# A two-layer graph network: rows of the middle passes made at the head of the turn that spreads them, and one square root for four blocks in the first pass

## The chip, the cores and the metric

The kernel runs on one core of a Trainium2 chip. A core has five engines with a queue of instructions each: TensorE (PE, matmuls), VectorE (DVE), ScalarE (ACT), GpSimd (POOL) and SyncE (SP), which here only issues DMA transfers. An engine takes its instructions in order; an instruction that has to wait holds up all behind it on its engine. The metric is the device time of one execution in microseconds, the median over several.

## The reference

The input is a table `x` of 32768 rows of 128 f32 numbers and 524288 edges (`src`, `dst`), sorted by `dst`. Two layers follow one another:

```python
# layer 0: x1 = layernorm(x + L0(x))
agg = segment_sum(x[src], dst)           # sums of neighbours' rows
h_local = bn(x + mlp((1 + eps) * x + agg))
h_attn  = bn(x + attention(x))           # 64 groups of 512 rows, 8 heads
L0 = bn(h + ffn(h)),  h = h_local + h_attn
# layer 1: out = layernorm(x1 + L1(x1)), three steps:
q = x @ Wq.T + bq
retrieved = softmax(q @ keys.T) @ values            # 512 keys
agg[row] += (dinv * x)[col];  lap = x - dinv * agg
x = 0.5 * x + 0.5 * (retrieved - 0.2 * lap)
# then layernorm(x, ln_w, ln_b)
```

So each of the three steps of layer 1 is, for each row, `0.4 x + 0.5 retrieved + 0.1 dinv agg`. The edges are the same in all of them.

## The kernel before, in words

The work of layer 1 is cut into 64 blocks of 512 rows (`NB` blocks of `BLK` rows, of `NCH` = 4 chunks of 128). Sums over neighbours are made by exchange through DRAM: rows are *spread* into slots ordered by the window of 128 rows that they go to, written to DRAM (`slots`), and in the next pass read back and *summed* per window. Both are matmuls with 0/1 matrices. So layer 1 is four passes:

- the first pass (pool `l1p`): makes layer 0's last normalisation, and spreads its rows;
- two middle passes (`l1w`, the loop over `t`): each sums what the pass before has spread, which ends a step, and spreads the new rows;
- the last pass (`l1z`): sums, and makes the two last normalisations.

A pass can't begin its sums before the pass ahead has written its last slots, as a window's slots come from all blocks.

What one block goes through, by the functions that hold it:

- `first` (first pass only): `load` fetches the block of layer 0's output (`vT`) and of the input (`x1`), `scale` applies batch norm on ACT, `turn` transposes on PE and adds on DVE, `norm` is a layer norm: mean and variance on DVE, square root on ACT (L1083), reciprocal and scaling on DVE (L1087, L1089), and a write of the rows to DRAM for the last pass.
- `consume` (middle and last pass): four windows of 19 matmuls each into a PSUM tile `seg` (5 with rows fetched singly by POOL, `listed`, 2 `common`, 12 with slots, `y_i`), each closed by three DVE instructions (L2103) that give the new rows `xn`. The 0/1 matrix of a window, `oh`, is one DVE instruction.
- `prepare`: the rows times `dinv` (`nx`), cut into three bf16 parts on ACT and DVE in turn (`rows`, `split_steps`: cast, subtract, cast, subtract, then a write to DRAM); the transposed rows `xT` (four transposes on PE, a copy on ACT) and the query `qT` (a matmul, then ACT).
- `emit`: scores against the keys, softmax (maximum on DVE, `Exp` on ACT), transposes, the product with the values, and the part of the step that needs no sums, `part_o`, to DRAM; and 24 times `spread`: two matmuls into a two-bank PSUM tile `exp`, and a cast of it to bf16 `y_o` by ACT or DVE (L1449). In the first pass every second cast is DVE's, in the middle passes every fourth. After each three casts SP writes half a window's slots.

There are two `exp` tiles in PSUM, so a pair of spreading matmuls waits for the cast of the pair before the last. In the middle passes there is one PSUM tile for query and scores together, and one for transposes.

The loop runs in turns, one block further each. In the first pass of before, turn n loads block n+3, does `first` of block n+2, `prepare` of block n+1 and `emit` of block n. In a middle pass, turn n sums block n+2, prepares block n+1 and spreads block n. Each step has a place number; `placed` sorts the steps of a turn by it, `weave` mixes the sums' steps evenly between them. This is the order of tracing. The order in each engine's queue is then set by a scheduler that works with priorities in order of tracing and its own estimates of readiness; layer 0 and the last pass switch it off (`manual_schedule`), the first and middle passes don't.

`Sqrt` and `Exp` lie in different tables of ACT; the compiler puts a table load ahead of each change.

Of the kernel before, what the change touches and what calls it, by code (L numbers as in the profile page):

```python
# [9 lines left out]
F32 = mybir.dt.float32  # L10
# [3 lines left out]
AF = mybir.ActivationFunctionType  # L14
OP = mybir.AluOpType
# [4 lines left out]
P = 128  # L20
D = 128
BLK = 512
NCH = BLK // P
# [885 lines left out]
def tile_gnn_resnorm(ctx: ExitStack, tc: tile.TileContext, a: dict, out: bass.AP):  # L909
# [8 lines left out]
    nc = tc.nc  # L918
    N = a["x"].shape[0]
    E = a["src"].shape[0]  # L920
    NB = N // BLK
# [38 lines left out]
    eps_c = cp.tile([P, 1], F32, name="eps_c")  # L960
# [9 lines left out]
    v = {n: vec[:, k:k + 1] for k, n in enumerate(VECS)}  # L970
# [984 lines left out]
    def layer1_grid(v_d, s3, c3):  # L1955

        exs = [Exchange("src", slots_d[t % 2], rows_d[t]) for t in range(T_STEPS)]
        with tc.tile_pool(name="l1g", bufs=1) as gp:
# [6 lines left out]
                if w < NW:  # L1965
                    picked[w] = exs[0].known_pick(wp, w)

            def first(b, st, wp, p_tr):


                def load():
                    st["v"] = wp.tile([P, BLK], F32, name="vT")
                    nc.sync.dma_start(st["v"], v_d[b])
                    st["x0"] = wp.tile([P, NCH, D], F32, name="x1")
                    nc.sync.dma_start(st["x0"], rows_of(a["x"], b))

                def scale():
                    nc.scalar.activation(st["v"], st["v"], AF.Identity, bias=c3, scale=s3)

                def turn():  # L1980
                    st["x"] = wp.tile([P, NCH, D], F32, name="xn", bufs=5)
# [10 lines left out]
            def prepare(t, b, st, wp, p_s, p_tr):  # L1992

                ex = exs[t]

                def rows():
                    nx = wp.tile([P, NCH, D], F32, name="nx")
                    nc.vector.tensor_tensor(nx, st["x"], dinv[:, b * NCH:(b + 1) * NCH].unsqueeze(2)
                                            .to_broadcast([P, NCH, D]), OP.mult)
                    st["r"], st["split"] = ex.split_steps(wp, b, nx, nx)  # L2000

                def project():
                    ps = p_tr.tile([P, NCH, P], F32, name="tr")
                    for c in range(NCH):
                        nc.tensor.transpose(ps[:, c, :], st["x"][:, c, :], ident)
                    st["xT"] = wp.tile([P, BLK], F32, name="xT")
                    nc.scalar.copy(st["xT"], ps.rearrange("p c n -> p (c n)"))

                def query():
                    ps = p_s.tile([P, BLK], F32, name="s")  # L2010
                    nc.tensor.matmul(ps, w["WqT"], st["xT"], start=True, stop=True)
# [121 lines left out]
            with tc.tile_pool(name="l1p", bufs=2) as wp, \  # L2133
                    tc.tile_pool(name="l1p_exp", bufs=2, space=PSUM) as p_e, \
                    tc.tile_pool(name="l1p_s", bufs=2, space=PSUM) as p_s, \
                    tc.tile_pool(name="l1p_tr", bufs=2, space=PSUM) as p_tr:
                sts, firsts = {}, {}
                for w0 in range(2):
                    ask_pick(wp, w0)
                for n in range(-3, NB):  # L2140
                    b = n + 3
                    if b < NB:
                        sts[b] = {}
                        load, firsts[b] = first(b, sts[b], wp, p_tr)
# [36 lines left out]
            with tc.tile_pool(name="l1z", bufs=2) as wp, \  # L2181
                    tc.tile_pool(name="l1z_r", bufs=1, space=PSUM) as p_r, \
                    tc.tile_pool(name="l1z_seg", bufs=4, space=PSUM) as p_g:
                t = T_STEPS - 1
                ramp = ramp_in_psum(p_r)
                with tc.manual_schedule():
# [3 lines left out]
                    for b in range(NB):  # L2190
                        st = {}
# [84 lines left out]
```

## Time and profile before

| | |
|---|---|
| median of 3 runs | 13,724.5 us (13,710.27 to 13,725.8) |
| profiled execution, its own time | 13,720.72 us |
| its span, first to last instruction | 13,718.8 us |
| granted TensorE clock, mean | 0.948 |
| PE busy over the span | 85% |
| DVE, ACT, POOL busy | 74%, 49%, 39% |

The stages of the span, in microseconds from its start, by the first and last instruction of each: attention, sorting of the edges and layer 0 until 6250; the first pass of layer 1 from 6256 to 7708; the two middle passes to 9883 and to 12,027; the last pass to the end.

How to read the lines of the profile: a group is line, engine, operation, output and inputs, shapes and count, then busy microseconds and the mean nanoseconds of one, then the idle time of the engine ahead of these instructions and what ended it. A wait line names who waited for whom, the sum in microseconds, how often, and the longest. A timeline line begins with start and length in microseconds. An f32 matmul appears as two rows. A matmul's end is modelled, and matmuls overlap, so their starts say more than their lengths.

### The profile page before, as it was taken

Reading aid. Unit: us, or ns where it says so; the run is one execution under the profiler, and the core shown is the slowest. Engines: PE = TensorE matmul, PEld = TensorE weight load, DVE = VectorE, ACT = ScalarE, POOL = GpSimd, SP = SyncE. Lnnn points to the kernel's source line nnn. Section 1 sums busy time; section 2 is a strip of 40 time slices with the busy share of each in tenths; the row PEclk is TensorE's granted clock in tenths of the full one; section 3 lists DMA queues with packets and bytes.
Section 4 is the critical chain, followed back from the end, with each engine's and each line's share of the span. In section 5 each row is a group of like instructions: output and inputs, shape, how many; then the busy total and the mean of one; then the engine's idle time right before and its main releaser. Section 6 shows DMA issues by size and latency. Waiting matters only on the chain. (4 is left out here: it accounts for less than half of the span.)

```text
span 13718.8 us, 167775 instructions
## 1 busy us (share of the span) xinstructions
PE 11728.4 (85%) x58924; PEld 5767.8 (42%) x58984; DVE 10087.5 (74%) x16572; ACT 6762.4 (49%) x10444; POOL 5314.5 (39%) x5333
## 2 busy tenths in 40 slices
PE   8988898887777888888999799999899999966666
PEld 3333333333333444444444455555455555533333
DVE  6998898879997777767888666666566666566666
ACT  4444444448884111137888566666566666600000
POOL 0000000000003777720000366666566666567777
PEclk9999999999999999999999999999999999988777
DMA  1000000007778999967888899999999999988887
GB/s 41 13 11 12 18 13 11 14 34 277 273 294 312 314 314 315 314 229 261 304 311 310 315 402 401 398 399 399 357 400 400 398 398 401 378 302 289 288 291 256
DMA packets 1339021, 3590.33 MB, mean 262 GB/s; under 512 B 197298, under 2 KB 579154, under 8 KB 1337010
## 3 DMA queue, kind: packets, MB, share of 16 engines
q1 hardware_dynamic: 968816, 2936.78, 56.6%
q0 software_dynamic: 252608, 520.41, 11.9%
q10 hardware_dynamic: 116738, 122.29, 2.6%
q8 instruction: 465, 7.62, 0.2%
q14 instruction: 394, 3.23, 0.1%
HBM read 2075.81 MB, written 1502.97 MB: 261 GB/s over the span
## 5 line engine op out<-in xcount | busy, mean ns | idle before, releaser
L1462 POOL DMA_INDIRECT listed<-rows,other x5120 | 5169.1, 1010 | 4103.9 <-issue 3140.6
L1449 ACT CAST y_o<-exp 128x768 bf16<-128x768 f32 x4352 | 3317.6, 807 | 984.7 <-PE exp L1444 732.6
L1444 PE MATMUL exp<-rows,pick 128*128 128x384 bf16 x12288 | 2818.7, 329 | 414.7 <-ACT y_o L1449 247.9
L1487 PEld LDWEIGHTS <-oh 128*128 128x128 bf16 x19456 | 1982.9, 102 | 2664.4 <-issue 1608.4
L1487 PE MATMUL seg<-y_i,oh 128*128 128x384 bf16 x12288 | 2643.7, 346 | 20.0 <-DMA y_i<-slots 18.7
L1449 DVE CAST y_o<-exp 128x768 bf16<-128x768 f32 x1792 | 1711.3, 955 | 688.9 <-PE exp L1444 576.7
L1444 PEld LDWEIGHTS <-pick 128*128 128x128 fp8e4 x12288 | 1203.3, 98 | 2054.3 <-issue 1371.6
L1487 PE MATMUL seg<-listed,oh 128*128 128x384 bf16 (+1 forms) x5120 | 1303.5, 335 | 885.5 <-DMA listed<-rows,other 848.3
L1390 POOL MEMSET rows<- 128x8 bf16 x64 | 6.8, 107 | 4022.2 <-DMA attn_d<-aT 2859.3
L1639 ACT ACTIVATE pT<-s 128x1024 f32<-128x1024 f32 x1024 | 1027.5, 1025 | 999.5 <-PE s L1614 859.7
L2103 DVE SCALAR_TENSOR_TENSOR part_i<-seg,dinv,part_i 128x128 f32<-128x128 f32 x1536 | 532.6, 347 | 1331.9 <-PE seg L1487 1320.8
L1619 DVE TENSOR_REDUCE mx<-s 128x2 f32<-128x1024 f32 x1024 | 1239.9, 1222 | 312.4 <-PE s L1614 308.4
L1614 PE MATMUL s<-k,q 32*128 32x512 f32 x4096 | 1196.7, 665 | 89.3 <-ACT pT L1639 82.0
L1635 PE MATMUL s<-ql,k 32*128 32x512 f32 x4096 | 1129.4, 646 | 63.8 <-DVE ql L1629 36.1
L1083 ACT ACTIVATE ln_rs<-ln_mv,eps_c 128x4 f32<-128x4 f32 x192 | 57.2, 298 | 1642.2 <-DVE ln_mv L1081 1641.5
L2028 PE MATMUL s<-keysT,qT 128*128 128x512 f32 x1536 | 796.0, 600 | 2.7 <-ACT pr L1062 1.7
L1432 DVE TENSOR_SCALAR_CACHE_REDUCE pick<-row_p,lane 128x512 fp8e4<-128x512 f32 x768 | 555.2, 748 | 260.2 <-PE row_p L1421 243.9
L2040 PE MATMUL s<-pt,values 128*128 128x512 f32 x1536 | 725.9, 595 | 10.7 <-ACT pt L2035 10.4
L1473 DVE TENSOR_TENSOR oh<-iota,slot 128x2432 bf16<-128x2432 bf16 x512 | 724.6, 1415 | 3.0 <-DMA slots<-y_o 3.0
L1473 DVE TENSOR_TENSOR oh<-ramp_p,slot 128x2432 bf16<-128x2432 bf16 x512 | 724.2, 1415 | 3.4 <-DMA slots<-y_o 3.4
L1487 PE MATMUL seg<-common,oh 128*128 128x384 bf16 (+1 forms) x2048 | 632.8, 351 | 69.1 <-DMA common<-rows,shared 68.6
L1421 PE MATMUL row_p<-row,ident_b 128*128 128x512 bf16 x1476 | 587.1, 398 | 95.7 <-DVE pick L1806 88.9
(404 smaller groups left out, 14138.6 us busy)
## 6 DMA issues: line engine op xcount, KB each, us to landing
slots<-y_o SPq DMA_DIRECT2D x2048, 576.0 KB
y_i<-slots SPq DMA_DIRECT2D x1024, 1152.0 KB
pick<-pick SPq DMA_DIRECT2D x1024, 192.0 KB
listed<-rows,other POOLq DMA_INDIRECT x5120
rows<-rows SPq DMA_DIRECT2D x192, 384.0 KB
part_d<-part_o SPq DMA_DIRECT2D x192, 256.0 KB
part_i<-part_d ACTq DMA_DIRECT2D x192, 256.0 KB
rows<-rows SPq DMA_DIRECT2D x64, 386.0 KB
```

Of the source, the lines that this page charges most:

```text
L1421: nc.tensor.matmul(ps, gc["ident"][:, w % P:w % P + 1].to_broadcast([P, P]), self.row[:, w // P, j * BLK:(j + 1) * BLK], start=True, stop= ...
L1444: nc.tensor.matmul(ps[:, j, :ROW], pick[:, o:o + P], r, start=True, stop=True)
L1449: (nc.vector.tensor_copy if to_dve else nc.scalar.copy)(dst, ps[:, :, :ROW])
L1462: nc.gpsimd.indirect_dma_start(out=g[:, k, :], out_offset=None, in_=self.table, in_offset=bass.IndirectOffsetOnAxis(ap=index[:, k:k + 1], ...
L1473: nc.vector.tensor_tensor(oh.rearrange("p c (w z) -> p c w z", z=2), ramp.rearrange("p (w z) -> p w z", z=2)[:, None].to_broadcast([P, NC2 ...
L1487: nc.tensor.matmul(ps[:, :n], oh[:, j, :], src, start=(k == 0), stop=(k == NC2 - 1))
L1614: nc.tensor.matmul(ps[:, s % 2, :], t["q", o][32 * s:32 * s + 32, c * P:(c + 1) * P], t["k", o][32 * s:32 * s + 32, :], start=True, stop=True)
L1619: nc.vector.tensor_reduce(m[:, c, 2 * i:2 * i + 2, xr[o]], st[b].pop(("two", i)), AX.X, OP.max, negate=True)
L1635: nc.tensor.matmul(ps[:, s % 2, :], t["k", o][32 * s:32 * s + 32, c * P:(c + 1) * P], t["ql", o][32 * s:32 * s + 32, :], start=True, stop= ...
L1639: nc.scalar.activation(t["p", c][:, 2 * i:2 * i + 2, :], ps, AF.Exp)
L2028: nc.tensor.matmul(s, st["q"][:, c * P:(c + 1) * P], keysT, start=True, stop=True)
L2040: nc.tensor.matmul(ps, values[:, k, :], st["pt"][:, k, :], start=(k == 0), stop=(k == NCH - 1))
```

## The change

There are two changes, in the first pass and in the middle passes.

In the first pass, `norm` is cut in two. `moments` makes mean and variance of a block into a tile that holds four blocks, and with the fourth block makes one square root and one reciprocal for all of them (16 columns). `norm` scales a block by them. So that the four blocks are there, the loop begins with turn -7 instead of -3: turn n loads block n+7, does `scale`, `turn` and `moments` of block n+6, `norm` of block n+2, and `prepare` and `emit` as before. `vT` has three buffers, `x1` eight.

In the middle passes turn n now sums block n+1, and both prepares and spreads block n. All steps of `prepare` come ahead of `emit`'s, in the order rows, the four steps of the split, transposes, query. There are 65 turns instead of 66 in a pass.

```diff
-            def first(b, st, wp, p_tr):
+            def first(b, st, wp, p_tr, group):
+                k = b % NCH
...
+                def moments():
+                    if k == 0:
+                        group["mv"] = wp.tile([P, NCH, NCH, 2], F32, name="ln_mvs")
+                    st["mv"] = group["mv"]
+                    t = wp.tile([P, NCH, 6], F32, name="ln_st")
+                    for c in range(NCH):
+                        nc.vector.bn_stats(t[:, c, :], st["x0"][:, c, :])
+                        nc.vector.bn_aggr(st["mv"][:, k, c, :], t[:, c, :])
+                    if k == 0:
+                        group["rs"] = wp.tile([P, NCH, NCH], F32, name="ln_rss")
+                    st["rs"] = group["rs"]
+                    if k == NCH - 1:
+                        nc.scalar.activation(st["rs"], st["mv"][:, :, :, 1], AF.Sqrt, bias=eps_c)
+                        nc.vector.reciprocal(st["rs"], st["rs"])
+
                 def norm():
-                    layer_norm(wp, st["x0"], st["x"])
+                    st["x"] = wp.tile([P, NCH, D], F32, name="xn", bufs=5)
+                    for c in range(NCH):
+                        nc.vector.tensor_scalar(st["x"][:, c, :], st["x0"][:, c, :], st["mv"][:, k, c, 0:1],
+                                                st["rs"][:, k, c:c + 1], op0=OP.subtract, op1=OP.mult)
                     nc.sync.dma_start(kept_of(xs_d[0], b), flat(st["x"]))
-                return load, [(7, scale), (12, turn), (15, norm)]
+                return load, [(7, scale), (12, turn), (15, moments)], [(14, norm)]
...
+                if at_once:
+                    return [(-1, f) for f in (rows, lambda: st["split"][0](), lambda: st["split"][1](),
+                                              lambda: st["split"][2](), lambda: st["split"][3](), project, query)]
                 return [(1, rows), (2, project), (4, lambda: st["split"][0]()), (7, query),
...
-                for n in range(-3, NB):
-                    b = n + 3
+                for n in range(-NCH - 3, NB):
+                    b = n + NCH + 3
...
-                    if n + 2 in sts:
-                        lists.append(firsts.pop(n + 2))
-                    if n + 1 in sts:
+                    if n + NCH + 2 in firsts:
+                        lists.append(firsts.pop(n + NCH + 2))
+                    if n + 2 in norms:
+                        lists.append(norms.pop(n + 2))
+                    if 0 <= n + 1 < NB:
                         lists.append(prepare(0, n + 1, sts[n + 1], wp, p_s, p_tr))
...
-                    for n in range(-2, NB):
+                    for n in range(-1, NB):
                         lists = []
-                        if n + 1 in sts:
-                            lists.append(prepare(t + 1, n + 1, sts[n + 1], wp, p_s, p_tr))
                         if n >= 0:
+                            lists.append(prepare(t + 1, n, sts[n], wp, p_s, p_tr, True))
                             lists.append(emit(t + 1, n, sts[n], wp, p_e, p_s, p_tr, 4))
                         two_b = placed(*lists)
-                        b = n + 2
+                        b = n + 1
```

More of the change, by code (lines that the diff above doesn't have):

```diff
@@ L1966, in ask_pick @@
                     picked[w] = exs[0].known_pick(wp, w)
-            def first(b, st, wp, p_tr):
+            def first(b, st, wp, p_tr, group):
+                k = b % NCH
                 def load():
-                    st["v"] = wp.tile([P, BLK], F32, name="vT")
+                    st["v"] = wp.tile([P, BLK], F32, name="vT", bufs=3)
                     nc.sync.dma_start(st["v"], v_d[b])
-                    st["x0"] = wp.tile([P, NCH, D], F32, name="x1")
+                    st["x0"] = wp.tile([P, NCH, D], F32, name="x1", bufs=2 * NCH)
                     nc.sync.dma_start(st["x0"], rows_of(a["x"], b))
@@ L1980, in turn @@
                 def turn():
-                    st["x"] = wp.tile([P, NCH, D], F32, name="xn", bufs=5)
                     ps = p_tr.tile([P, NCH, P], F32, name="tr")
@@ L1985, in turn, with prepare @@
                     nc.vector.tensor_add(st["x0"], st["x0"], ps)
+                def moments():
[12 more added lines that the diff above has]
+                        nc.vector.reciprocal(st["rs"], st["rs"])
                 def norm():
-                    layer_norm(wp, st["x0"], st["x"])
+                    st["x"] = wp.tile([P, NCH, D], F32, name="xn", bufs=5)
+                    for c in range(NCH):
+                        nc.vector.tensor_scalar(st["x"][:, c, :], st["x0"][:, c, :], st["mv"][:, k, c, 0:1],
+                                                st["rs"][:, k, c:c + 1], op0=OP.subtract, op1=OP.mult)
                     nc.sync.dma_start(kept_of(xs_d[0], b), flat(st["x"]))
-                return load, [(7, scale), (12, turn), (15, norm)]
-            def prepare(t, b, st, wp, p_s, p_tr):
+                return load, [(7, scale), (12, turn), (15, moments)], [(14, norm)]
+            def prepare(t, b, st, wp, p_s, p_tr, at_once=False):
                 ex = exs[t]
@@ L2136, in layer1_grid @@
                     tc.tile_pool(name="l1p_tr", bufs=2, space=PSUM) as p_tr:
-                sts, firsts = {}, {}
+                sts, firsts, norms, group = {}, {}, {}, {}
                 for w0 in range(2):
                     ask_pick(wp, w0)
-                for n in range(-3, NB):
-                    b = n + 3
+                for n in range(-NCH - 3, NB):
+                    b = n + NCH + 3
                     if b < NB:
                         sts[b] = {}
-                        load, firsts[b] = first(b, sts[b], wp, p_tr)
+                        load, firsts[b], norms[b] = first(b, sts[b], wp, p_tr, group)
                         load()
                     lists = []
-                    if n + 2 in sts:
-                        lists.append(firsts.pop(n + 2))
-                    if n + 1 in sts:
+                    if n + NCH + 2 in firsts:
[3 more added lines that the diff above has]
+                    if 0 <= n + 1 < NB:
                         lists.append(prepare(0, n + 1, sts[n + 1], wp, p_s, p_tr))
```

## The prediction

> **What bounds the kernel now.** I read the busy time by stage first, then the groups and waits of the two stages that the diff touches, then the timelines of single turns. A turn is one pass of the loop over blocks of 512 rows. The stages, as microseconds, then busy time and instructions of each engine, clock, DMA share, GB/s:
>
> ```profile
> 6256.00:7708.00 1452.00, 1300.34 (x6002) 689.23 (x6002) 1252.41 (x2342) 1271.70 (x2103) 0.00 (x0) 1.00 0.84 305
> 7708.00:9883.00 2175.00, 2075.41 (x10638) 1159.39 (x10639) 1309.08 (x2115) 1352.17 (x2240) 1416.77 (x1341) 0.99 1.01 390
> 9883.00:12027.00 2144.00, 2059.82 (x10610) 1152.99 (x10610) 1302.68 (x2110) 1352.78 (x2241) 1355.38 (x1283) 1.00 1.01 392
> ```
>
> In the first pass PE, DVE and ACT are all at 86 to 90%: three engines that hand two PSUM buffers (`exp`) round, none of them full. In the middle passes PE is at 95%. The groups of the first pass on ACT, and what DVE waits for there:
>
> ```profile
> L1062 ACT ACT_TABLE_LOAD x63 | 80.8, 1283 | 1.1
> L1083 ACT ACT_TABLE_LOAD x62 | 79.5, 1283 | 1.1
> ...
> L1083 ACT ACTIVATE ln_rs<-ln_mv,eps_c 128x4 f32<-128x4 f32 x64 | 19.1, 298 | 2.5 <-DVE ln_mv L1081 1.8
> ```
> ```profile
> DVE y_o L1449 <- PE exp L1444: 138.5, 212, 1.7
> DVE nm L1060 <- PE s L2028: 36.3, 71, 1.4
> ```
>
> The reader is to see 125 table loads, two per block (to Sqrt, back to Exp): 160 us of ACT's 1272. ACT's timeline shows how they stand in its queue:
>
> ```profile
> 6918.74 1.28 ACT L1083 ACT_TABLE_LOAD   x1
> 6920.04 0.30 ACT L1083 ACTIVATE ln_rs<-ln_mv,eps_c 128x4 f32<-128x4 f32 x1
> 6920.25 0.80 ACT L1449 CAST y_o<-exp 128x768 bf16<-128x768 f32 x1
> ```
>
> A steady middle turn, PE by start:
>
> ```profile
> 8810.23 1.13 PE L2011 MATMUL s<-xT,w_WqT 128*128 128x512 f32 x2
> 8811.19 1.63 PE L1487 MATMUL seg<-y_i,oh 128*128 128x384 bf16 x9
> ...
> 8815.86 0.81 PE L1444 MATMUL exp<-rows,pick 128*128 128x384 bf16 x4 [0.29 <-ACT y_o L1449]
> 8817.23 0.48 PE L1444 MATMUL exp<-rows,pick 128*128 128x384 bf16 x2 [0.56 <-ACT y_o L1449]
> ```
>
> From start to start a 384-column matmul takes 0.162 us, a 512-column f32 one 0.86, a transpose 0.11. A turn has 76 `seg`, 48 `exp`, 9 f32 products and 24 transposes: 12.3 + 7.8 + 7.7 + 2.6 = 30.4 us. Turns in 8400 to 9400 last 32.7 to 34 (mean 32.9), and what is missing is mostly `exp` waiting for a cast. DMA moves 399 GB/s there, but PE waits for it only 6 us in 1200 (8200 to 9400).
>
> The ends of the passes, on PE:
>
> ```profile
> 7707.49 0.48 PE L1444 MATMUL exp<-rows,pick 128*128 128x384 bf16 x2 [0.72 <-DVE y_o L1449]
> 7719.44 0.48 PE L1487 MATMUL seg<-listed,oh 128*128 128x384 bf16 x1 [11.47 <-DMA listed<-rows,other]
> ...
> 7781.69 0.52 PE L1444 MATMUL exp<-rows,pick 128*128 128x384 bf16 x2
> ```
>
> 74 us pass with no `exp`: 11.5 until the first rows come, then sums of two whole blocks, limited by gathers. In the next pass it is 49.7 us (9882.9 to 9932.65). At the other end, 9821.8 to 9882.9, two blocks are spread with almost no sums beside them.
>
> **The skill.** The page "ScalarE: Activation LUTs", section "What ACT_TABLE_LOAD costs", puts a change of table set at 1283 ns of load plus about 1380 of drain, 2.66 us. The trace has the 1283, but from load to next instruction only 1.30 us (6918.74 to 6920.04); I go by the trace, so half of the page's price. "Perfetto Trace Analysis", section "Identifying the Most-Contended Engine", says that matmul occupancy doesn't measure how full PE is; here one `seg` shows 326 ns while they start 162 apart, so I count starts.
>
> **Part 1, first pass: one Sqrt for four blocks.** Removed: 48 Sqrt (about 0.2 us each from start to start), 48 reciprocals on DVE (0.17), and table loads: the compiled order has 39 where it had 133, so 94 x 1.30 = 122 us off ACT's queue; with the Sqrts 132 us, 2.1 per turn. Added: nothing but longer-lived buffers (`x1` 8, `vT` 3). Moved: loads of `vT` and `x1` (two SP issues of 0.34 us, 256 KB each) go four turns earlier; their buffers are free, so SP's queue doesn't stop. The norms keep their turn, but in the compiled order the norms of a group (16 x 0.25 us) now stand close together on DVE.
>
> What a load costs: laid over all loads from 6660 to 7560, DVE idles 24% of the 1.3 us of the Sqrt load and 25% of the 1.2 after it (0.6 us), 13% of 1.5 us after the Exp load (0.2), and half of the 2 us that begin 6 us after it (1.0), when ACT's casts and exponentials lie back to back. So 0.8 us per turn directly, 1.8 at most. Below, DVE is the floor: 1252/64 = 19.6 us per turn of 22.7. In three turns of four 0.8 to 1.8 goes: 38 to 86 us. I take 60. Late next is DVE. If its bunched norms delay casts, I leave 0 to 30 us of loss in the range. The head: four blocks must be through before the first norm, three more than now, DVE 0.68 + 0.9 + 0.7 us each, some 7 us; the last turns are lighter by the same work: +4. Sum **-56**.
>
> **Part 2, one turn less between sums and spreading (two passes).** *Ends.* First `exp` comes after sums of one block, not two. First middle pass: 11.5 + 28 (four windows, 7719.4 to 7747.5) + 6.5 for the new head below = 46 instead of 74: -28. Second: four windows are done at 9909.65, so 9916 instead of 9932.65: -16. The drain has one lone block instead of two, but one more full turn is run: lone ones take 30 each (61 us for two), a full turn 32.9, and the sums of three quarters of a block are left over where before there were none: before 62 x 32.9 + 2 x 30.5 = 2101 from first to last `exp`, after 62.75 x 32.9 + 1.25 x 30 = 2102. To it come about 5 us for the head of the last block, which nothing covers. -28 + 5 - 16 + 5 = **-34**. The last `rows` write (SP, 384 KB) is issued one turn later, still some 20 us before the pass ends, so the gathers on POOL's queue find it landed.
>
> *Steady turn.* I timed its head by hand along the compiled order, with latencies from the trace (PE to ACT or DVE 0.21, the others 0.05). t = 0 is the last `seg` of the block. DVE closes it with a one-hot (1.33) and a cast between: `xn` at 3.3, `nx` at 3.9. PE meanwhile has 26 `seg` of the next windows and 8 `exp` of the old block. ACT: casts, `rows` at 5.4, `xT` to 6.5; PE, ready at 6.15, waits 0.4 for it. Query to 7.5, `qT` to 8.4; behind two `seg` the first score waits 0.6. Behind `qT` on ACT the second `rows` cast ends at 8.9, DVE's last subtraction at 9.7, just when PE asks for the new rows. With small waits 1.3 us by then, another 0.8 in the rest of the turn, 32.6 in all, where the shortest turns are now 32.7. The jitter of now (mean 32.9) makes it 32.8; f32 products that follow a wait took 0.96 instead of 0.86, and two more of them do so: 33.0; and as I left out casts that wait for a write to `slots`, I take 33.1, +0.2 us per turn, for 126 turns: **+25**; bounds -0.3 (windows now end 8 to 9 us apart, not 4 to 12, which evens the fetches) and +1.0 (the query wait and the score wait both uncovered): -38 to +126.
>
> Sum: -56 - 34 + 25 = -65. The profiled execution took 13,720.7 around a span of 13,718.8; the median is 13,724.5, 4 us above. Forecast on the median: 13,724.5 - 65, about **13,658 us**.
>
> **Rivals.**
> - *ACT alone binds the first pass*: the full 132 us come off. For it: ACT idles only 2.2 us per turn. Against: DVE idles as little. 13,724 - 132 + 4 - 34 + 25: 13,587.
> - *The loads are hidden*, DVE binds: nothing in part 1, and the ends pay for the head. For it: during the Exp loads DVE doesn't idle at all. 13,724 + 4 - 34 + 25: 13,719.
> - *Slower: the head of the middle turn.* PE has one buffer for query and scores, and the chain `xn`, `xT`, query, `qT`, score lies in one turn, behind a one-hot and casts. At 1.3 us more per turn it is +164 - 90 = 13,798; it decides from 90/126 = 0.7 us per turn. For it: nothing but `seg` covers the chain, and ACT casts in order. Against: the hand timing, and that 34 matmuls stand in the gap.
> - That the change doesn't do what it says: the compiled order excludes it for the loads.
>
> **How the numbers follow.** Forecast 0.52 (13,620 to 13,695), full gain 0.13, hidden 0.17, longer turn 0.18. A measurement tells about 0.2% (27 us) from no change. Faster: 0.52 + 0.13 + 0.03 of the third = 0.68; same: 0.13, nearly all of the third; slower: 0.19. The range runs from 13,565 (beyond most of the full gain) to 13,765 (half of the longer turn).
>
> **What would show it.** First pass 1396 us (7708 now), turns near 21.5; some 31 table loads in it; DVE's wait for `exp` below 100 us. Middle: from the last `exp` of one pass to the first of the next 46 and 34 us; the query's wait for `xT` 0.4 and the score's for `qT` 0.6 per turn; turn 32.9 to 33.3. Wrong I am if the turn is above 33.6, or the first pass keeps 22 us per turn.

## The result: slower by 0.4%, and where the time went

The changed kernel takes 13,778.2 us (median of 5 runs, 13,756.41 to 13,793.19) where the kernel before took 13,722.73 beside it (13,710.27 to 13,725.8): ratio 1.0043, interval 1.0032 to 1.0054. The forecast was 13,658, faster.

The three stages of the changed kernel, by the same view as before (microseconds, then busy time and instructions of PE, PEld, DVE, ACT and POOL, clock, DMA share, GB/s):

```profile
6236.00:7673.00 1437.00, 1291.95 (x5996) 685.34 (x5996) 1248.29 (x2285) 1148.49 (x1962) 0.00 (x0) 1.00 0.84 307
7673.00:9885.00 2212.00, 2100.60 (x10636) 1143.46 (x10637) 1321.30 (x2114) 1344.86 (x2240) 1418.27 (x1335) 0.99 1.01 383
9885.00:12064.00 2179.00, 2088.62 (x10612) 1138.62 (x10612) 1316.76 (x2110) 1345.43 (x2241) 1370.99 (x1290) 0.99 1.01 386
```

ACT's busy time in the first pass has fallen by 123 us and the pass only by some 15. PE's share in the middle passes is still 95%, in passes that are 37 and 35 us longer. To compare the kernels I count a first pass from the first transpose of `vT` to the last `exp`, and in a middle pass apart the gap ahead of its first `exp` and the spreading, from the first `exp` to the last, in which 64 blocks are spread in every version:

| us, from the PE timelines of the profiled executions | before | after | difference | forecast |
|---|---|---|---|---|
| first pass | 1460.7 | 1445.1 | -15.6 | -56 |
| gap ahead of the first middle pass's `exp` | 74.2 | 54.3 | -19.9 | -28 |
| gap ahead of the second's | 50.2 | 39.4 | -10.8 | -16 |
| spreading, first middle pass | 2100.7 | 2158.4 | +57.7 | +18 |
| spreading, second middle pass | 2094.3 | 2139.5 | +45.2 | +18 |
| sum | | | +56.6 | -64 |

(The +18 are 1 for the changed drain, 5 for the uncovered last head and half of the 25 for the steady turn.) The medians differ by 55.5 us, so the table holds the whole of it. In short, the first pass and the gaps won 46 us where 100 were forecast, and the spreading lost 103 where 36 were forecast. (All ahead of the first pass took 20 us less in this one execution, with the same instructions; in another profile of the same kernel it took 6 less. The last pass is the same within 2.)

**First pass.** The groups of table loads, and what DVE, ACT and PE wait for (the sum in us, how often, the longest):

```profile
L1062 ACT ACT_TABLE_LOAD x16 | 20.5, 1283 | 0.3
L2001 ACT ACT_TABLE_LOAD x15 | 19.2, 1283 | 0.3
L2001 ACT ACTIVATE ln_rss<-ln_mvs,eps_c 128x16 f32<-128x16 f32 x16 | 4.9, 307 | 0.2
```
```profile
ACT y_o L1449 <- PE exp L1444: 191.4, 287, 1.9
DVE y_o L1449 <- PE exp L1444: 117.4, 211, 1.4
...
PE exp L1444 <- DVE y_o L1449: 48.1, 79, 0.8
```

and, of the kernel before, the line that the prediction does not show:

```profile
ACT y_o L1449 <- PE exp L1444: 136.5, 212, 2.5
```

There are 31 loads where 125 were, just the number foreseen. But ACT is now idle for 108 us more than before (123 less the 15 of the pass), and about half of that is its wait for `exp`, 191 us instead of 136. DVE's wait for `exp`, 138.5 before, fell by 21, which is close to what the pass won.

**The ends**, on PE:

```profile
7672.31 0.48 PE L1444 MATMUL exp<-rows,pick 128*128 128x384 bf16 x2 [0.72 <-DVE y_o L1449]
7684.40 0.48 PE L1487 MATMUL seg<-listed,oh 128*128 128x384 bf16 x1 [11.60 <-DMA listed<-rows,other]
...
7718.14 0.48 PE L1487 MATMUL seg<-listed,oh 128*128 128x384 bf16 x1 [2.06 <-DMA listed<-rows,other]
...
7723.85 1.02 PE L2031 MATMUL s<-xT,w_WqT 128*128 128x512 f32 x2
...
7726.61 0.81 PE L1444 MATMUL exp<-rows,pick 128*128 128x384 bf16 x4
```

The first `exp` now stands behind one block's sums, but their gathers (`listed`) hold PE until 7718.1, 34 us after the first rows, where I had taken 28 from the old trace; from there to the `exp` it is 8.5.

**The head of a middle turn.** The waits that I had forecast at the query and the first score:

```profile
9786.27 1.12 PE L2031 MATMUL s<-xT,w_WqT 128*128 128x512 f32 x2 [0.25 <-ACT xT L2027]
9787.30 0.48 PE L1487 MATMUL seg<-y_i,oh 128*128 128x384 bf16 x2
9788.17 1.12 PE L2051 MATMUL s<-keysT,qT 128*128 128x512 f32 x2 [0.39 <-ACT qT L2033]
```

They are there and as large as forecast. What I had not looked at is the DMA side. Waits over 1600 us (8200 to 9800) of the kernel before:

```profile
DVE y_o L1449 <- PE exp L1444: 120.8, 100, 2.0
...
ACT y_o L1449 <- DMA slots<-y_o: 31.1, 59, 1.5
DVE y_o L1449 <- DMA slots<-y_o: 30.2, 35, 2.2
...
DVE nm L1060 <- PE s L2028: 13.2, 30, 1.0
...
PE seg L1487 <- DMA y_i<-slots: 4.3, 8, 1.2
```

and of the changed kernel, the same stretch:

```profile
ACT y_o L1449 <- DMA slots<-y_o: 269.2, 98, 5.6
DVE y_o L1449 <- PE exp L1444: 215.6, 142, 4.0
DVE nm L1060 <- PE s L2051: 190.5, 106, 3.7
...
PE seg L1487 <- DMA y_i<-slots: 23.3, 18, 3.2
```

Casts on ACT wait nearly nine times as long for a write of `slots` to free its buffer. PE itself waits 23.3 us instead of 4.3 for reads of `slots`, 0.4 us more per turn. Over the steady part of both middle passes turns have a mean of 33.7 us (32.9 before) and go up to 38.4 (34.9 before). The DMA view of 8200 to 9800, all packets and then the largest queue (packets, MB, share of the 16 engines), before:

```profile
DMA packets 205033, 638.58 MB, mean 399 GB/s; under 512 B 30586, under 2 KB 71244, under 8 KB 204918
...
q1 hardware_dynamic: 150302, 526.83, 83.2%
```

and after:

```profile
DMA packets 199798, 622.25 MB, mean 389 GB/s; under 512 B 29816, under 2 KB 69473, under 8 KB 199684
...
q1 hardware_dynamic: 146497, 513.36, 82.5%
```

The rate fell by 2.5%, but a turn moves the same bytes, so this only says that turns are longer. What is new is that the share of q1 hardly fell with it: a packet there took 0.832 x 16 x 1600 us / 150302 = 141.7 ns before and 144.2 after.

The f32 products changed too. One score, with no wait shown ahead of it, and the instruction behind it, before:

```profile
8813.30 1.02 PE L2028 MATMUL s<-keysT,qT 128*128 128x512 f32 x2
8814.16 0.81 PE L1444 MATMUL exp<-rows,pick 128*128 128x384 bf16 x4
```

and after:

```profile
8813.99 1.12 PE L2051 MATMUL s<-keysT,qT 128*128 128x512 f32 x2
8814.95 0.49 PE L1444 MATMUL exp<-rows,pick 128*128 128x384 bf16 x2
```

From start to start that is 0.86 us before and 0.96 after. From 7900 to 9780, 206 of 223 scores took 0.96 after, 25 of 228 before.

### The profile page after: what moved, and what is told of

Read it like the earlier page. It is cut to its first block, busy times and chain, and to the rows that moved or that the text cites. A ratio compares the mean times of both kernels' runs of the same rounds, so it can differ in the third digit from the quotient of the medians.

```text
span 13754.6 us, 167969 instructions
## 1 busy us (share of the span) xinstructions
PE 11754.5 (85%) x58924; PEld 5729.0 (42%) x58984; DVE 10110.6 (74%) x16524; ACT 6624.6 (48%) x10302; POOL 5328.2 (39%) x5333
## 5 line engine op out<-in xcount | busy, mean ns | idle before, releaser
L1487 PE MATMUL seg<-y_i,oh 128*128 128x384 bf16 x12288 | 2750.1, 346 | 61.3 <-DMA y_i<-slots 60.4
L1487 PE MATMUL seg<-listed,oh 128*128 128x384 bf16 (+1 forms) x5120 | 1260.9, 334 | 869.9 <-DMA listed<-rows,other 838.9
L1635 PE MATMUL s<-ql,k 32*128 32x512 f32 x4096 | 1123.4, 642 | 64.4 <-DVE ql L1629 35.8
L1060 DVE TENSOR_REDUCE nm<-s 128x1 f32<-128x512 f32 x768 | 527.2, 689 | 539.5 <-PE s L2051 537.5
L2051 PE MATMUL s<-keysT,qT 128*128 128x512 f32 x1536 | 844.1, 632 | 32.4 <-ACT qT L2033 28.4
```

The lines of the kernel that those rows point to most:

```text
L1487: nc.tensor.matmul(ps[:, :n], oh[:, j, :], src, start=(k == 0), stop=(k == NC2 - 1))
L1635: nc.tensor.matmul(ps[:, s % 2, :], t["k", o][32 * s:32 * s + 32, c * P:(c + 1) * P], t["ql", o][32 * s:32 * s + 32, :], start=True, stop= ...
L2051: nc.tensor.matmul(s, st["q"][:, c * P:(c + 1) * P], keysT, start=True, stop=True)
```

## The experiments

The runs came in batches, each on one chip with the kernel before beside them. In three batches (e1 to e4, e9 to e12, e13 to e16) the stages that move most data took longer, those that no edit touches as well, and times are compared within a batch only. I call this the lower memory rate, after the GB/s in the rows below; its cause is not known. Some of the expectations speak of a slow chip, but the rate did not stay with the chip: chip 6 had e5 to e8 at the higher rate and e13 to e16 at the lower, chip 12 e9 to e12 at the lower and e17 and e18 at the higher. Spread is the mean time of the two spreadings, in the profiled execution.

| run | time, us | before in the batch | ratio | first pass | spread |
|---|---|---|---|---|---|
| the profile of before, and the change | 13,778 | 13,723 | 1.0043 [1.0032, 1.0054] | 1460.7, 1445.1 | 2097, 2149 |
| e5_changed | 13,789 | 13,724 | 1.0050 [1.0034, 1.0067] | 1443.8 | 2155 |
| e6_before_picks | 13,820 | 13,724 | 1.0070 [1.0050, 1.0090] | 1459.9 | 2146 |
| e7_changed_picks | 14,010 | 13,724 | 1.0208 [1.0188, 1.0229] | 1441.9 | 2272 |
| e8_first_dve10 | 13,686 | 13,724 | 0.9970 [0.9958, 0.9983] | 1419.0 | 2105 |
| e17_query_first_dve10 | 13,738 | 13,714 | 1.0020 [1.0010, 1.0029] | 1419.6 | 2156 |
| e18_ahead_at_once | 13,762 | 13,714 | 1.0036 [1.0022, 1.0050] | 1444.3 | 2131 |
| e1_first_only | 14,856 | 14,869 | 0.9990 [0.9982, 0.9999] | 1446.3 | 2399 |
| e2_middle_only | 14,647 | 14,869 | 0.9856 [0.9839, 0.9874] | 1461.2 | 2295 |
| e3_changed_y3 | 14,918 | 14,869 | 1.0041 [1.0026, 1.0055] | 1444.9 | 2439 |
| e4_before_y3 | 15,071 | 14,869 | 1.0140 [1.0122, 1.0159] | 1461.0 | 2501 |
| e9_ahead_at_once | 15,093 | 14,699 | 1.0270 [1.0249, 1.0292] | 1444.4 | 2519 |
| e10_query_first | 14,491 | 14,699 | 0.9857 [0.9838, 0.9876] | 1446.1 | 2264 |
| e11_changed_y3 | 14,784 | 14,699 | 1.0054 [1.0035, 1.0074] | 1446.1 | 2394 |
| e12_first_dve8 | 14,697 | 14,699 | 0.9995 [0.9986, 1.0005] | 1459.4 | 2316 |
| e13_ahead_at_once | 15,099 | 14,680 | 1.0288 [1.0267, 1.0310] | 1446.3 | 2514 |
| e14_query_first | 14,521 | 14,680 | 0.9889 [0.9870, 0.9908] | 1446.2 | 2262 |
| e15_middle_only | 14,544 | 14,680 | 0.9903 [0.9883, 0.9922] | 1460.6 | 2269 |
| e16_query_first_dve10 | 14,492 | 14,680 | 0.9871 [0.9851, 0.9892] | 1417.5 | 2254 |

### The first pass alone, and what bounds it

`e1_first_only` is the kernel before with `first`, its call and the first pass's loop as in the change.

> The first pass of the changed kernel, with the middle passes of before. If the whole loss comes from the middle passes (their two stages took 2213 and 2179 us in the profile of the changed kernel, 2175 and 2145 before), this kernel is 10 to 25 us faster than before, all of it in the first pass (1445 us from first transposes to last spreading matmul, 1461 before), and its middle passes last 2175 and 2145 us. If the earlier start of that stage in the changed kernel (6227 us, 6247 before) belongs to the change, it is seen here again, and the gain is 35 us.

First pass 1446.3 us, as in the changed kernel at either memory rate (1441.9 to 1446.3), against 1459.9 to 1461.2 for the old one. So the -15 us is part 1's, and it is the same at both rates.

Why so little? The next two also change which engine casts, so that DVE has 10 or 8 of a block's 24 casts instead of 12 (middle passes of before; not shown: there the call has 6 in place of 4, which under the new rule is again every fourth cast):

```diff
-                    ex.spread(wp, p_e, "exp", i, picked[i], st["r"][:, c, :], m, y, n % share == share - 1)
+                    ex.spread(wp, p_e, "exp", i, picked[i], st["r"][:, c, :], m, y, (n + 1) * share // 24 != n * share // 24)
-                        lists.append(emit(0, n, sts[n], wp, p_e, p_s, p_tr, 2))
+                        lists.append(emit(0, n, sts[n], wp, p_e, p_s, p_tr, 10))
```

> The changed first pass with the middle passes of before, and in the first pass 10 of a block's 24 casts on DVE instead of 12. Theory: DVE (19.6 us of work per turn) bounds the first pass once the table loads are gone, which is why 122 us of loads gave 16 us. Two casts less are 1.7 us of DVE's turn, ACT has them free: the first pass falls from 1445 to 1350 to 1390 us. Rival: the alternation over two PSUM buffers bounds it, and two casts in a row on ACT make it wait more: within 20 us of 1445, or longer.

> The changed first pass with 8 of 24 casts on DVE (10 of 24 gave 1419 us, 12 of 24 1445), middle passes of before. If DVE still bounds, another 20 to 30 us come off: 1390 to 1400. If ACT (17.8 us of work per turn, and 0.7 for each cast taken over: 20.6) now binds, it is 1410 to 1450.

Stage rows of the first pass (1420 us of it), with 10 casts on DVE:

```profile
6240.00:7660.00 1420.00, 1317.28 (x6008) 683.24 (x6009) 1144.94 (x2190) 1216.50 (x2093) 0.00 (x0) 0.99 0.86 313
```

and with 8:

```profile
6560.00:7980.00 1420.00, 1287.96 (x5886) 678.60 (x5887) 1022.54 (x2003) 1276.86 (x2179) 0.00 (x0) 1.00 0.84 304
```

With 10 the pass takes 1419.0 us, 25 less than with 12, and the kernel is faster than the one before: 0.997. With 8 it takes 1459.4. PE's wait for DVE's casts, 48.1 us with 12, is with 10 (6240 to 7660):

```profile
PE exp L1444 <- DVE y_o L1449: 14.0, 20, 1.3
```

So with 12 DVE's casts were late. With 8 ACT has the most work, 90% of the stretch, and I take it to be the late one; no wait shows that as plainly. DVE has 17.9 us of work per block at 10, ACT 19.0, and the block takes 21.9, so no engine is full. Argued, and not shown apart, is the reason: the two take casts in a fixed alternation out of two `exp` tiles, so ACT, with its loads gone, can't take what DVE is behind with. The 1350 to 1390 us that I had expected at 10 did not come. 10 casts with the table loads left in were not tried.

### The change of the middle passes

`e5_changed` is the changed kernel once more, in another batch; `e2_middle_only` and `e15_middle_only` have the old first pass with the changed loop over `t` and `prepare`.

> The changed kernel as it is, beside the kernel before on the same chip. The first four runs fell on a chip where the kernel before takes 14,869 us instead of 13,723, and there the new middle passes alone made it 1.4% faster, where the changed kernel had been 0.4% slower. If that belongs to the chip, this kernel is slower by 0.3 to 0.5% where the kernel before takes 13.7 ms, and faster by 1.2 to 1.8% where it takes 14.9 ms. If what was seen there came from leaving the first pass as it was, it is slower on either.

> The first pass of before, with the middle passes of the changed kernel. If the two parts don't act on one another, this is slower than before by the loss of the middle passes, 70 us (0.5%), and the first pass lasts 1461 us as before. If a part of the loss is something that the first pass hands on, it is well below 70 us.

> Old first pass, changed middle passes. If the two parts add: first pass 1461 us, middle passes 2212 and 2185, 15 us above the changed kernel: 13,795 where before takes 13,723 (ratio 1.005 to 1.006). On the chip where before takes 14,868 the same kernel was 1.4% faster than before; if the sign goes with the chip's memory rate, it is slower here when before takes 13,723 and faster when before takes 14,700 or more.

The loss repeats: spreading 2158 and 2151 us. But in the slower batches the same change of the middle passes is a gain of 1.0 to 1.4%. (The middle passes changed alone ran only at the lower rate, and the whole change only at the higher.) Layer 0 (4000 to 6000) and the middle pass (8200 to 9800), with the old middle passes in the slow batch (e1_first_only):

```profile
4000.00:6000.00 2000.00, 1468.40 (x6653) 737.67 (x6668) 1262.24 (x2692) 411.65 (x749) 1097.46 (x1164) 0.89 0.80 271
8200.00:9800.00 1600.00, 1424.90 (x7144) 791.15 (x7142) 873.74 (x1419) 912.08 (x1503) 938.40 (x883) 0.96 0.97 354
```

with the changed ones there (e2_middle_only):

```profile
4000.00:6000.00 2000.00, 1463.88 (x6650) 738.80 (x6666) 1265.26 (x2694) 415.43 (x752) 1097.05 (x1163) 0.89 0.80 271
8200.00:9800.00 1600.00, 1468.11 (x7394) 792.74 (x7393) 915.02 (x1466) 941.48 (x1563) 1010.03 (x914) 0.99 1.00 367
```

and at the higher rate, the kernel before:

```profile
4000.00:6000.00 2000.00, 1601.41 (x7680) 834.76 (x7697) 1480.40 (x3125) 456.29 (x837) 1256.46 (x1327) 0.94 0.90 307
8200.00:9800.00 1600.00, 1559.06 (x8049) 873.26 (x8047) 990.84 (x1600) 1024.85 (x1697) 1055.37 (x990) 1.00 1.03 399
```

Layer 0, the same in all three, moves 271 GB/s instead of 307. In the middle pass the old order falls from 399 to 354, the changed one from 389 only to 367: a turn grows from 32.9 to 37.5 us in the one, from 33.7 to 35.8 in the other. So the sign of the middle passes' change goes with the memory rate. The first pass takes the same time at both rates.

Three things keep the lower rate from being explained. It isn't shown that transfers as such are slower: in layer 0 the DMA share fell with the rate, from 0.90 to 0.80, and a packet of q1 took 146.4 ns (55.6% x 16 x 2000 us / 121499) instead of 140.7 (60.9%, 138479), 4% more where 12% less was moved. The granted clock is lower as well (0.89 and 0.94, in the old middle pass 0.96 and 1.00), too little for a turn that is 14% longer. And the waits of these traces can't be read, because they lack more than half of the records of transfers that land: in e1 there are 12,704 from 8200 to 9800, in the kernel before 30,552. So for the lower rate I use times, rates and shares only.

### The lead or the placing

The change does two things to a middle turn: a block is prepared in the turn that spreads it (the lead of one turn is lost), and all steps of `prepare` stand at the turn's head. `ahead_at_once` keeps the lead and places the steps at the head:

```diff
-                    for n in range(-1, NB):
+                    for n in range(-2, NB):
                         lists = []
+                        if n + 1 in sts:
+                            lists.append(prepare(t + 1, n + 1, sts[n + 1], wp, p_s, p_tr, True))
                         if n >= 0:
-                            lists.append(prepare(t + 1, n, sts[n], wp, p_s, p_tr, True))
                             lists.append(emit(t + 1, n, sts[n], wp, p_e, p_s, p_tr, 4))
...
-                        b = n + 1
+                        b = n + 2
```

> The changed first pass; in the middle passes all steps of prepare at the head of the turn, as in the change, but for the block that the next turn spreads: the distance of two turns between sums and spreading stays. Where the kernel before takes 13.72 ms: if the loss is the chain xn, xT, query, qT, score within one turn, it isn't on the path here, the turn is 32.7 to 33.0 us and the kernel 10 to 20 us faster than before. If it is the bunching of the steps (casts and subtractions side by side on ACT and DVE, fewer fetches in time), the turn is 33.6 to 33.9 and the kernel 90 to 110 us slower than before, as the ends are not shortened.

> Changed first pass; middle passes with the steps of prepare together at the head of the turn, as in the change, but one turn ahead of the spreading, as before (so the head's chain is waited for by nobody). Theory 'the lead': the turn grows by 0.9 us because rows and scores wait for a chain of the same turn; with the lead back the turn is 32.9 us again and the first gaps are 74 and 50 us, so 13,705 on a chip on which before takes 13,723 (ratio 0.999). Theory 'the clustering': casts and slots writes are held up by what stands together at the head of ACT's and DVE's queues, lead or not; then the turn stays at 33.5 or above and the time at 13,790 or above (ratio 1.005 or more).

> Changed first pass, steps of prepare together at the head of the turn, one turn ahead of the spreading as before. At the higher memory rate (before at 13,720): theory 'the lead' 32.9 us per turn and 13,705 (0.999); theory 'the clustering' 33.5 or more and 13,790 or more (1.005). At the lower rate (before at 14,680) 1.028 again, as measured, with turns of 39 us.

At the higher rate (e18) the spreading takes 2139.5 and 2122.7 us: 67 of the 103 us by which the changed kernel spreads longer are there although the lead is back. Scatter is to be kept in mind: e8, whose middle passes are those of before, spread in 16 us more than before in the two passes together. At the lower rate this kernel is the slowest of its batches, with turns of 39.5 us. Waits and DMA of e18, 8200 to 9800:

```profile
ACT y_o L1449 <- PE exp L1444: 108.0, 250, 0.8
...
ACT y_o L1449 <- DMA slots<-y_o: 80.6, 123, 3.3
...
DVE y_o L1449 <- DMA slots<-y_o: 51.1, 41, 3.6
...
PE seg L1487 <- DMA y_i<-slots: 7.5, 18, 1.0
```
```profile
DMA packets 200672, 625.28 MB, mean 391 GB/s; under 512 B 29929, under 2 KB 69701, under 8 KB 200558
...
q1 hardware_dynamic: 147210, 516.05, 83.5%
```

So the long waits for `slots` alone are not what sets the turn: here they are half of the changed kernel's (132 us against 272), and the turn is 33.5. Nor are PE's waits for reads of `slots`, 7.5 us against 23.3. A packet of q1 took 145.2 ns here, as in the changed kernel (144.2) and unlike the old order (141.7; 141.8 in e8).

### Query first

`query_first` is the changed kernel with one line of `prepare` turned round:

```diff
-                    return [(-1, f) for f in (rows, lambda: st["split"][0](), lambda: st["split"][1](),
-                                              lambda: st["split"][2](), lambda: st["split"][3](), project, query)]
+                    return [(-1, f) for f in (project, query, rows, lambda: st["split"][0](), lambda: st["split"][1](),
+                                              lambda: st["split"][2](), lambda: st["split"][3]())]
```

and with `dve10` it also has the first pass of e8.

> The changed kernel with transposes and query traced ahead of the rows in prepare: in the compiled order the copy xT stands ahead of the first rows cast on ACT, and one matmul or none between query and score where there were two. If the head's chain makes the loss, the query's wait goes (0.35 us per turn) and the score's grows from 0.55 to at most 0.9: the turn stays within 0.2 us of 33.8. If the rows behind it are what PE waits for, the turn grows by 0.5 us, 60 us in all.

> The changed kernel with transposes and query traced ahead of rows and split. Theory 'head waits': query and score waits (0.25 to 0.55 us each per turn) are most of the 0.9 us; with the query first they go, rows come later, the turn is 33.0 to 33.3 and the time 13,700 to 13,740 where before takes 13,723 (ratio 0.999 to 1.001). Theory 'DMA': the turn is set by how fast slots are written and read, PE's waits only move to other instructions, the turn stays at 33.6 to 33.9 and the ratio at 1.004 to 1.006.

> Query first as in the run beside it, and in the first pass 10 of 24 casts on DVE instead of 12. First pass 1419 us as measured with the old middle (26 less). If query first brings the turn to 33.2: 13,680 where before takes 13,723 (ratio 0.997); if the turn stays at 33.7: 13,760 (ratio 1.003).

> Changed kernel, query traced ahead of rows, 10 of 24 casts of the first pass on DVE. At the higher memory rate (before at 13,720): theory 'head waits', middle turn 33.0 to 33.3, time 13,680 (ratio 0.997); theory 'DMA', turn 33.6 to 33.9, time 13,750 (1.002). At the lower rate (before at 14,680) 0.987 again, as measured.

At the higher rate (e17) the first pass has its 1419.6 us, but the turn stays at 33.8, as the theory "DMA" forecast. But the waits at the head did not go either, as the table below shows: query and score together wait 1.06 us instead of 0.93. So this run doesn't decide between the two theories. Waits of e17, 8200 to 9800:

```profile
ACT y_o L1449 <- DMA slots<-y_o: 256.2, 92, 4.8
...
PE s L2051 <- ACT qT L2033: 26.1, 39, 0.8
...
PE seg L1487 <- DMA y_i<-slots: 9.6, 8, 2.9
```

PE's time beyond its own work, from start to start less 0.1625 us per 384-column matmul, 0.43 per f32 row and 0.11 per transpose, for 7900 to 9780, in us per turn:

| | before | after | e17, query first | e18, lead kept |
|---|---|---|---|---|
| ahead of the query | 0.15 | 0.36 | 0.12 | under 0.04 |
| ahead of a score | 0.00 | 0.57 | 0.94 | 0.29 |
| ahead of `exp` | 1.77 | 1.40 | 1.76 | 1.95 |
| ahead of `seg` with slots | 0.24 | 0.76 | 0.30 | 0.36 |
| all | 2.4 | 3.2 | 3.2 | 3.1 |

The f32 products' own lengthening is in the sum (0.5 us per turn after, 0.1 before), most of it in the rows of `exp` and `seg`. Take the query's wait away and the score's grows by more (0.37 for 0.24); give the lead back and the waits stand ahead of `exp` again; the sum stays. At the lower rate query first is about as good as the changed middle passes are in any case (0.986 and 0.989 against 0.986 and 0.990).

### Two attempts to give the DMA room

A third `y_o` buffer in the middle passes (`y3`) lets a cast go on while two writes are under way. And `picks` fetches the 0/1 matrix `pick` once per block instead of for each window, 0.59 MB of some 13 MB less per turn; it leaves out three of four fetches, so three windows of a block are spread with another window's matrix, and only the time counts.

```diff
-                st["y"] = wp.tile([P, 2, KS, ROW], BF16, name="y_o")
+                st["y"] = wp.tile([P, 2, KS, ROW], BF16, name="y_o", bufs=self.y_bufs)
...
-                    picked[w] = exs[0].known_pick(wp, w)
+                    picked[w] = picked[w - 1] if w % every else exs[0].known_pick(wp, w)
```

> The changed kernel with three buffers instead of two for the cast rows y_o of the middle passes. Theory: casts wait for the writes of slots of the window before the last (ACT 316 us in 2040 us of the first middle pass, 113 us on ACT and DVE before), because the new order spreads the windows' pairs in quicker succession; then these waits go, the turn falls from a mean of 33.9 to 33.3 us, and the kernel is 60 to 90 us faster than the changed one, about as fast as before. Rival: the DMA engines are full (388 GB/s, share 1.01) and would only shift the wait to the reads of slots; then the time stays within 20 us of the changed kernel, and PE's waits for y_i rise from 27 us to over 100.

> The kernel before with the same third y_o buffer in the middle passes. If its turn of 32.7 us is set by PE and the casts, the 113 us of waits per pass for slots are mostly beside the path, and 0 to 20 us are gained. If writes of slots set its pace too, 50 us or more.

> The changed kernel with a third y_o buffer again, now beside its neighbours of this call. On the slow chip it was 0.4% slower than before, where the new middle passes with two buffers had been faster. Where the kernel before takes 13.72 ms: if casts that wait for writes of slots make half of the loss, the turn falls to 33.3 us and the kernel gets level with before. If a third buffer lets more writes stand in the DMA queues ahead of the reads of slots, the turn is longer than 33.8 us, and waits for slots give place to waits of other kinds.

> The kernel before, with less data moved: in the middle passes the 0/1 matrix of spreading is fetched once per block instead of once per window (the output is wrong by it): 0.59 of 13.1 MB per turn less, 4.5%, 12 DMA issues fewer. If DMA sets the turn, it falls by 4.5% (32.9 to 31.5 us, or on the slow chip 37.5 to 35.8), 190 to 220 us in all. If PE and the casts set it, it falls by less than 0.3 us, under 40 us in all.

> The changed kernel with the same fetches left out (wrong output). If its lost 0.9 us per turn were the waits of the head alone (query for xT 0.35, score for qT 0.55), the turn stays at its shortest value of 33.2 us. If DMA waits (y_i 0.7 us per turn, writes of slots) make the mean of 33.8, they go, and the turn falls to 33.2 but not below. If DMA sets the pace, 32.3.

All five are slower than their batch's kernel before. The third buffer ran at the lower rate only, where the traces don't show whether it took the waits for `slots` away; the kernel before is 1.4% slower with it. At the higher rate, where the waits had been seen, it was not tried. With less to fetch the turn of the kernel before is 33.6 to 34.0, at 374 GB/s and a DMA share of 1.01. So fewer bytes alone did not shorten the turn, and the DMA share stayed at 1 with fewer bytes to move. Each of these edits also changed the compiled order, so none is a clean removal of one cost. That holds for all edits of the middle passes: every one that ran at the higher rate (the change, query first, the lead kept, `picks`) gave a longer turn than the order before, 33.5 us or more against 32.9. No run tells steps at the head of the turn from any other reordering of it.

## Why the prediction was wrong, step by step

Of the 121 us between the forecast and the result of the table, 67 lie in the spreading, 40 in the first pass and 13 in the gaps. Both signs of being wrong that the prediction named came: a turn of 33.7 us (above 33.6), and 22.3 us per turn in the first pass (above 22).

- **Part 1, the number of loads and their 1.30 us: right.** 31 loads, and ACT 123 us less busy (132 priced).
- **Part 1, what they are worth: the size was off, -15.6 for -56.** I laid DVE's idle time over the loads and took 0.94 us per turn as won. The rate of spreading, first to last `exp` over 64 blocks, went from 22.62 to 22.30 us per block; and the later first `exp` cost 5 (7 foreseen). So the term "I take 60" measured 20 us. Most of DVE's idle time beside a load did not go with it: it stands ahead of other `exp` now (117 us, where I had said below 100). "The loads are hidden" was the nearer case for this part. I had "late next is DVE" in the working, and e8 shows it: two casts fewer on DVE won 25 us.
- **Part 2, the ends: right in kind, 31 won of 44.** The missing part in the first gap lies mostly in gathers, 34 us for one block's instead of 28.
- **Part 2, steady turn: this step failed.** +0.2 us forecast, 0.8 measured. The waits that the hand timing gave for the query and the score (0.4 and 0.6) came out at 0.36 and 0.57. What failed is the line "another 0.8 in the rest of the turn", even with the 0.5 added to it for jitter, f32 products and writes: the rest had 2.2 us of waits before and kept 2.3. I took the time spent waiting at the head as time in which the rest catches up, as if only PE and the casts had to be served. Of the 2.3, two parts can be named: the longer f32 products grew by 0.4 us per turn (0.2 forecast, for two more of them; it was more than three), and PE's wait for reads of `slots`, for which the working has no term, by 0.4. Other waits, those ahead of `exp` above all, fell by about as much. That the query and score came out as timed doesn't save the step: in e18 they wait 0.3 us together, and the turn is still 33.5.
- Behind that stands a reading: "PE waits for it only 6 us", of DMA. In the table of stages the DMA share was 1.01 and I passed over it. The Trainium skill would have warned me: "Perfetto Trace Analysis", section "Roofline", says that a core alone is bounded by its 16 DMA engines at about 435 GB/s in all, some 120% of a 358 GB/s share; the middle passes ran at 399, 92% of that. Against a plain limit on bytes stands e6, with less to move and a longer turn. I had also left out, knowingly, the casts that wait for writes, at 0.1 us; they wait 4 to 5 us per turn more. In e18 they wait 1.5 us per turn more and the turn is nearly as long, so this is not the price by itself either.
- **The rival "slower: the head"** ended near in time (13,798 against 13,778), above its threshold of 0.7 us per turn. Its mechanism, the wait for query and score, is shown only in part: PE's time ahead of those two rose by 0.78 us per turn, but in e18 the score's rose by 0.29 only, the query's not at all, and the loss was still two thirds.

A slip in the working that changes nothing: 13,724.5 less 65 is 13,659.5.

So what is shown is where the loss lies, and that neither the query's and score's waits (e18), nor the casts' waits for `slots` (e18), nor the number of bytes (e6) make it alone. The cause stays open: why PE's waits add up to 3.1 to 3.2 us in each of three new orders and to 2.4 in the old, whether the packets of q1 (2% longer there) are cause or effect, and why at the lower memory rate the changed middle passes are a gain. That the lower rate comes from the other core of the pair at work is only a guess: the Trainium skill's "HBM Reference", section "Specifications (TRN2)", says that the two share a domain's bandwidth, about 358 GB/s each when both stream, and the middle passes moved 331 to 376 there; no run here shows the other core.

## What to carry to other kernels

When a loop's working counts only the waits that an edit adds, ask which of the old waits it takes to go, and why: here they stayed, and the turn grew by the new ones. An engine that seldom waits for DMA is no proof that transfers are free in another order; here PE's wait for reads of `slots` grew fivefold with the same bytes. Time taken off one of two engines that take work in a fixed alternation was worth little until the shares were set anew: two casts moved, with the loads gone, were worth more than 94 table loads. And measure an edit of a memory-heavy loop in more than one batch before keeping it: its sign can turn.

## What the runs showed that I had not expected

- The same kernel takes 13,714 to 13,724 us in some batches and 14,680 to 14,869 in others, on the same chips, with the difference in other stages than the first pass (layer 0 271 instead of 307 GB/s, first pass equal within 5 us); the changed middle passes alone won 1.0 to 1.4% in the slower, and the whole change lost 0.4 to 0.5% in the faster.
- Steps at the head of a turn with the lead kept: 1.0036 at the higher rate, 1.027 and 1.029 at the lower. There, in the slowest kernel, the DMA share of the middle pass is 0.89 to 0.90, where it is 1.02 at the higher rate.
- A third buffer for a tile whose writers wait for its transfers made the kernel slower (1.014, at the lower rate).
